# Two graph layers in one kernel: layer norms on ScalarE, their scale and shift vectors folded into weights or applied on GpSimd, and later weights loaded one by one

## The chip, the cores and the metric

The kernel runs on one core of a Trainium2 chip. The core has TensorE (PE) for matrix products, which accumulate in PSUM; VectorE (DVE), ScalarE (ACT) and GpSimd (POOL) for elementwise work; and SyncE (SP), whose ordered queue issues every DMA of this kernel. Each engine takes its instructions in program order, and engines wait for each other by semaphores. The metric is the device time in microseconds, the median of several runs.

## The reference

There are 64 independent graphs of 256 nodes with 256 features, and an integer adjacency matrix (256 x 256) for each. Two layers follow each other; all biases are zero and all scale vectors one in the data, but the kernel computes with them.

```python
# layer 0: attention with 8 heads, masked by the adjacency value r = 0..3, then a feed-forward block
q, k = src @ Wq + bq, src @ Wk + bk                    # 8 heads of 32
attn = softmax(q k^T / sqrt(32))
out  = sum over r of (attn * (adj == r)) @ (src @ Wv[r] + bv[r])
x  = ln(src + out @ Wo + bo) * g1 + beta1
x  = ln(x + gelu(x @ W1 + b1) @ W2 + b2) * g2 + beta2   # 256 -> 1024 -> 256
# layer 1: two graph-attention products (softmax over axis 1), then a feed-forward block
h  = gat(gat(x, adj, W1, a1), adj, W2, a2)             # scores leaky_relu, adj <= 0 masked
h  = ln(x + h) * g_ln1 + b_ln1
y  = ln(h + relu(h @ w_ff1 + b_ff1) @ w_ff2 + b_ff2) * g_ln2 + b_ln2
```

So a graph has four layer norms. `ln(x)` is `(x - mean) / sqrt(var + eps)` over the 256 features of a node.

## The kernel before

A graph is worked on as a whole: 256 nodes are two chunks of 128 partitions, and everything is float32 but the masks. Class `Graph` splits one graph into some 190 named steps, each a method that issues one or a few instructions. The table `PLACES` gives every step a place in time on a scale on which graphs follow each other every `PERIOD` = 60 units, and a table covers some seven such periods. At the end all steps of all 64 graphs are sorted by place and issued in that order. So the program order of every engine is written out by hand or by a planner, some seven graphs are in flight at once, and what counts in the steady state is the order of the places modulo 60. Units of the table are not microseconds.

The steps that matter here, with `m` for a half of the heads, `h` for a head, `c` for a chunk:

- Attention: `load` (features and adjacency), `cast`, `jT` (a transposing DMA), `xT` (DVE transpose), `qk`, `qkc`, `s` (PE, 32-row tiles), `max` (DVE), `exp` (ACT), `rec`, `nrm` (ACT), `eT` (DVE transpose into `sq`), `eW` and `eR` (the transposed tile through a DRAM scratch and back), `ec` (ACT copy to PSUM), `pm` (DVE product with three masks), `pl` (GpSimd product with the fourth), `v` and `vc`, `po` (PE, 32-column tiles), `oT`, `wo`, `ya`.
- Norm 1 to 4: `st` (DVE statistics), `rt` (power -1/2 on GpSimd), `ln` (DVE). Norm 1 works on tile `y`, norms 2 and 3 on `ffa_res`, norm 4 on `ffb_res`. Norm 1 is followed by the feed-forward block `a`, norm 2 by the graph attention, norm 3 by the feed-forward block `b`, norm 4 by `store`.
- Feed-forward blocks (`a` with Gelu, `b` with Relu): `aT, aW, aR` (transposed input through DRAM), `ar` (GpSimd: residual plus bias row), `au0` to `au3` (PE, products with `W1`), `ax0` to `ax3` (ACT: bias and Gelu), `ad0` to `ad7` (PE, products with `W2`), `ae` (DVE: residual); `b` likewise.
- Graph attention: `hT, hW, hR`, `ga0, ga1` with copies `gac0, gac1`, `ipA` (PE: a row spread over partitions), `zA` (ACT), `zlA, zmA, zxA` (DVE), `zeA` (ACT, Exp), `zdA` (DVE), `h10, h11` with copies `h1c0, h1c1`, the same again from `ipB` to `zdB`, then `h2` and `h2a`.

Products of PE other than `s`, `ad` and `bd` go to PSUM tiles of one tag with two buffers, taken in turn: `ps_mm` (`qk`, `v`, `po`, `wo`, `ga`, `ip`, `h1`, `h2`, `au`, `bu`). A product can start only when the one before the last has been copied out by ACT or DVE.

The norm of before is two passes over each chunk on DVE:

```python
nc.vector.scalar_tensor_tensor(yc, yc, self.mv[:, c, 0:1], self.gain, op0=ALU.subtract, op1=ALU.mult)   # L289
nc.vector.scalar_tensor_tensor(yc, yc, self.rs[:, c:c + 1], self.shift, op0=ALU.mult, op1=ALU.add)      # L293
```

The weights that are needed first (`Wq`, `Wk`, `Wv`) are loaded ahead of everything, together with the features of graphs 0 and 1. All later ones (33 DMAs: `wo`, both feed-forward blocks, the graph-attention weights, vectors) are issued in one go at the place of `jT` of graph 0. `gat_weights`, which combines the graph-attention weights on PE and DVE, has place 120.

Of the kernel before, what the change touches and what calls it, by code (L numbers as in the profile page):

```python
# [9 lines left out]
F32 = mybir.dt.float32  # L10
# [7 lines left out]
P = 128  # L18
# [6 lines left out]

PERIOD = 60.0
PLACES = {
    "load": -11.99, "cast": -4.6, "xT": -2.51, "jT": 7.74, "qk0": 12.06, "qkc0": 12.47, "mask0": 35.2,
    "qk1": 41.83, "mask4": 42.97, "qkc1": 43.93, "s0": 50.23, "max01": 52.59, "max00": 53.97,
    "exp00": 59.92, "exp01": 60.39, "rec01": 63.35, "nrm01": 68.6, "max02": 70.93, "eT01": 71.05,  # L30
    "max03": 74.95, "v00": 75.04, "mask1": 75.2, "exp02": 75.84, "rec02": 76.61, "exp03": 76.62,
    "s1": 77.63, "mask2": 78.13, "nrm02": 78.17, "vc00": 81.45, "rec00": 83.14, "rec03": 85.5,
    "eW01": 87.08, "nrm03": 87.16, "eT02": 87.32, "eR01": 90.18, "max12": 91.51, "eW02": 92.34,
    "nrm00": 93.28, "max11": 93.62, "exp12": 93.89, "eT03": 95.13, "eR02": 96.16, "rec12": 96.86,
    "eT00": 97, "exp11": 97.55, "nrm12": 97.77, "v01": 98.23, "ec01": 98.98, "max10": 100.89,
    "vc01": 101.13, "exp10": 102.04, "max13": 102.21, "y": 102.21, "rec11": 102.55, "pm01": 102.88,
    "eW03": 102.97, "mask3": 103.29, "rec10": 103.36, "nrm11": 103.84, "ec02": 104.67, "eT12": 104.67,
    "eW00": 104.68, "v10": 104.89, "eT11": 105.49, "pl01": 105.96, "eR00": 106.25, "vc10": 106.55,
    "pm02": 107.2, "exp13": 107.77, "nrm10": 110.66, "rec13": 112.27, "pl00": 112.6, "pl02": 117.17,
    "v11": 117.37, "ec00": 117.67, "eR03": 117.75, "vc11": 118.97, "pm00": 121.14, "eW11": 121.82,  # L40
    "eR11": 122.22, "eW12": 125.9, "ec03": 128.07, "pm03": 128.9, "eT10": 129.4, "pl03": 131.19,
    "nrm13": 132.88, "eR12": 133.75, "eW10": 135.15, "ec11": 135.58, "po0": 137.43, "oT0": 138.17,
    "eT13": 138.22, "pm11": 140.7, "eR10": 141.05, "ec10": 143.46, "yb": 143.7, "pl11": 144.31,
    "eW13": 144.38, "pm10": 144.52, "pl10": 145.72, "ec12": 145.91, "eR13": 149, "pl12": 149.19,
    "pm12": 150.57, "ec13": 151.58, "pm13": 153.57, "pl13": 158.31, "po1": 158.56, "oT1": 159.13,
    "wo": 166.08, "ya": 168.05, "st1": 173.82, "rt1": 178.3, "ln1": 181.37, "aT": 186.38, "aW": 188.07,
    "aR": 190.12, "ar": 199.24, "au0": 199.52, "au1": 201.67, "ax0": 202.72, "ax1": 203.71, "au2": 206.84,
    "ax2": 207.11, "ad0": 208.42, "au3": 209.92, "ad1": 210.58, "ax3": 211.3, "ad2": 212.42, "ad3": 213.46,
    "ad4": 214.51, "ad5": 214.81, "ad6": 216.46, "ad7": 216.67, "ae": 218.37, "st2": 219.27, "rt2": 220.84,
    "ln2": 221.17, "hT": 221.8, "hW": 225.17, "hR": 225.65, "ga0": 227.46, "gac0": 229.51, "ga1": 231.81,  # L50
    "gac1": 232.91, "ipA": 233.38, "zA": 233.55, "zlA": 234.68, "zmA": 236.37, "zxA": 236.64, "zeA": 238.87,
    "zdA": 239.62, "h10": 246.26, "h11": 246.44, "h1c0": 246.81, "h1c1": 247.31, "ipB": 247.55,
    "zB": 248.29, "zlB": 256.22, "zmB": 256.91, "zxB": 258.84, "zeB": 259.12, "zdB": 261.65, "h2": 265.36,
    "h2a": 266.13, "st3": 268.5, "rt3": 268.87, "ln3": 273, "bT": 277.62, "bW": 280.27, "bR": 280.43,
    "bu0": 283.46, "bx0": 284.14, "bd0": 292.07, "bu1": 295.49, "bx1": 298.81, "bu2": 302.43, "bu3": 303.37,
    "bd1": 303.83, "bx2": 304.64, "bx3": 306.29, "bd2": 306.63, "bd3": 308.89, "bd4": 312.76, "bd5": 314.98,
    "bd6": 316.39, "br": 317.09, "bd7": 320.72, "be": 323.55, "st4": 352.74, "rt4": 364.85, "ln4": 370.31,
    "store": 411.06,
}

# [11 lines left out]
def kernel(  # L72
# [52 lines left out]
    def issue_loads():  # L125
        for t, src in loads:
            nc.sync.dma_start(t, src)
        loads.clear()

    def weight(w, name, mixed=False):  # L130

        k, n = w.shape[0] // P, w.shape[1]
        t = const.tile([P, k, n], F32, name=name)
        if mixed:
            mixed_rows(t, w)
        else:
            loads.append((t, w.rearrange("(k p) n -> p k n", p=P)))
        return t

    def mixed_rows(t, w):  # L140
        for a in range(A):
            loads.append((t[a::A], w.rearrange("(k a x) n -> a x k n", a=A, x=S)[a]))

# [10 lines left out]
    def load_front(g):  # L154

        xin = fp.tile([P, KD, N // S, S], F32, tag="xin", name=f"xin{g}", bufs=1)
        xs = x[g].rearrange("(b y) (k a x) -> a y k b x", y=S, a=A, x=S)
        for a in range(A):
            nc.sync.dma_start(xin[a * S:(a + 1) * S], xs[a])
        adi = fp.tile([P, C, N], I32, tag="adi", name=f"adi{g}", bufs=1)  # L160
        nc.sync.dma_start(adi, adj[g].rearrange("(c p) d -> p c d", p=P))
        return xin, adi
# [13 lines left out]
    issue_loads()  # L176
    loaded[1] = load_front(1)
# [7 lines left out]
    w1, b1_c = weight(W1, "w1", mixed=True), colvec(b1, FF, "b1_c")  # L185
    w2, b2_r = weight(W2, "w2"), rowvec(b2, D, "b2_r")
# [12 lines left out]
    f1, bf1_c = weight(w_ff1, "f1", mixed=True), colvec(b_ff1, FF, "bf1_c")  # L199
    f2, bf2_r = weight(w_ff2, "f2"), rowvec(b_ff2, D, "bf2_r")  # L200
    gl2_r, bl2_r = rowvec(g_ln2, D, "gl2_r"), rowvec(b_ln2, D, "bl2_r")

# [61 lines left out]

    class Norm:


        def __init__(self, gain, shift, name):
            self.gain, self.shift, self.name = gain, shift, name
# [15 lines left out]

        def apply(self):
            for c in range(C):
                yc = self.y[:, c, :]
                nc.vector.scalar_tensor_tensor(yc, yc, self.mv[:, c, 0:1], self.gain,  # L289
                                               op0=ALU.subtract, op1=ALU.mult)  # L290
            for c in range(C):
                yc = self.y[:, c, :]
                nc.vector.scalar_tensor_tensor(yc, yc, self.rs[:, c:c + 1], self.shift,  # L293
                                               op0=ALU.mult, op1=ALU.add)

    class Ffn:


        def __init__(self, wa, ba, func, wb, row, name):
            self.wa, self.ba, self.func, self.wb, self.row, self.name = wa, ba, func, wb, row, name  # L300
            self.x = Transposed(f"{name}_T", bp, "sT", 3)
            self.ps = {}

        def residual(self, src):
            self.r = bp.tile([P, C, D], F32, tag="res", name=f"{self.name}_res", bufs=4)
            nc.gpsimd.tensor_tensor(self.r, src, bc(self.row, [P, C, D]), ALU.add)
# [25 lines left out]
    class Graph:  # L332
# [147 lines left out]
        def residual_bias(self):  # L480
            nc.gpsimd.tensor_tensor(self.y, self.y, bc(bo_r, [P, C, D]), ALU.add)
# [87 lines left out]
        def operations(self):  # L569
# [3 lines left out]
            self.ffa = Ffn(w1, b1_c, AF.Gelu, w2, b2_r, f"ffa{g}")  # L573
            self.ffb = Ffn(f1, bf1_c, AF.Relu, f2, bf2_r, f"ffb{g}")
# [26 lines left out]
            for n, f, src in (("a", self.ffa, lambda: self.y), ("b", self.ffb, lambda: self.ffa.r)):  # L601
                ops[f"{n}T"] = lambda f=f, src=src: f.x.squares(src())
                ops[f"{n}W"], ops[f"{n}R"] = f.x.write, f.x.read
                ops[f"{n}r"] = lambda f=f, src=src: f.residual(src())
                for i in range(KF // 2):
                    ops[f"{n}u{i}"] = lambda f=f, i=i: f.up(2 * i)
                    ops[f"{n}x{i}"] = lambda f=f, i=i: f.act(2 * i)
                for i in range(KF):
                    ops[f"{n}d{i}"] = lambda f=f, i=i: f.down(i // 4, 2 * (i % 4))
                ops[f"{n}e"] = f.end  # L610
            for n, gain, shift, src in (("1", g1_r, be1_r, lambda: self.y), ("2", g2_r, be2_r, lambda: self.ffa.r),
                                        ("3", gl1_r, bl1_r, lambda: self.ffa.r),
                                        ("4", gl2_r, bl2_r, lambda: self.ffb.r)):
                norm = Norm(gain, shift, f"x{n}_{g}")
                ops[f"st{n}"] = lambda norm=norm, src=src: norm.stats(src())
                ops[f"rt{n}"] = norm.root
                ops[f"ln{n}"] = norm.apply
# [21 lines left out]
    plan = [(PLACES["jT"], len(PLACES), issue_loads), (2 * PERIOD, len(PLACES), gat_weights)]  # L639
# [36 lines left out]
```

## Time and profile before

| | value |
|---|---|
| time, median of 3 runs | 3756.78 us (3755.02 to 3757.12) |
| span of the profiled execution | 3744.0 us |
| mean granted TensorE clock | 0.989 |
| HBM traffic | 243 MB read, 201 MB written, 119 GB/s over the span |
| first store, last store issued | 310.8 us, 3740.8 us |

The page gives the busy time of each engine as a share of the span. It says how much work an engine has, not whether somebody waits for it; for that there are the waits and the timeline. A matmul record of float32 is half a product, since each product is issued as two. A row such as `x8` in the timeline is a run of eight records, and the time between the starts of two rows is what the first one cost on PE. The costliest groups on the four engines, from the page's list:

| line | engine, tile | count | busy us | mean ns |
|---|---|---|---|---|
| L450 | DVE `pm` | 512 | 891.7 | 1742 |
| L455 | GpSimd `pl` | 512 | 597.5 | 1172 |
| L326 | PE `ffb_po` | 2048 | 513.6 | 379 |
| L428 | ACT `e` (Exp) | 1024 | 473.4 | 470 |
| L438 | ACT `e` (normalise, in place) | 1024 | 462.0 | 503 |
| L306 | GpSimd `ffb_res` (residual plus row) | 64 | 84.1 | 1313 |

### The profile page before, as it was taken

The numbers are of one execution on the slowest core, as the hardware profiler recorded it, in microseconds if no ns is written. First come the engines' busy times: TensorE is split into PE (matmuls) and PEld (weight loads), VectorE is DVE, ScalarE is ACT, GpSimd is POOL, SyncE is SP. The second block draws the span as 40 slices with busy tenths as digits, with TensorE's granted clock in tenths as the row PEclk, the third lists the DMA queues.
The fourth block names the chain that finished last, engine by engine and source line by source line (L and its number), as shares of the span: only waits on it lengthen the run. The fifth ranks groups of instructions, "written<-read, shape, count | busy, mean of one in ns | idle before, by whom it ended". The sixth has DMA issues, their size and how long they took to land.

```text
span 3744.0 us, 65142 instructions
## 1 busy us (share of the span) xinstructions
PE 3614.4 (97%) x22808; PEld 2687.0 (72%) x22808; DVE 3246.3 (87%) x5896; ACT 2217.7 (59%) x6145; POOL 1548.2 (41%) x1350
## 2 busy tenths in 40 slices
PE   5999999999999999999999999999999999999997
PEld 3677777777777777777777777777777777777775
DVE  4889888988898898898889888988988988998884
ACT  3666656655656666666656566656666665666642
POOL 3444344443443443443444444434434434444430
PEclk7999999999999999999999999999999999999998
DMA  6444344344444443443443443444444434444331
GB/s 177 125 130 125 112 130 129 114 129 121 123 123 124 127 122 123 127 124 117 128 123 113 132 127 115 130 121 123 125 123 125 124 120 127 125 123 127 118 102 34
DMA packets 808568, 457.44 MB, mean 122 GB/s; under 512 B 332976, under 2 KB 717616, under 8 KB 808240
## 3 DMA queue, kind: packets, MB, share of 16 engines
q1 hardware_dynamic: 808240, 453.27, 41.2%
q8 instruction: 181, 2.97, 0.3%
q14 instruction: 147, 1.20, 0.1%
HBM read 243.42 MB, written 201.33 MB: 119 GB/s over the span
## 4 chain that ended last, share of the span: by engine, by line
PE 52%; DVE 35%; DMA 5%; issue 5%; ACT 2%; SPq 1%; POOL 0%; DVEq 0%; POOLq 0%; ACTq 0%
PE ffb_po L326 10%; PE ffa_ps L312 7%; PE po L467 6%; DVE pm L450 6%; PE v_ps L399 6%; PE ffb_ps L312 5%; DVE nmax L420 5%; DVE ffa_res L293 4%; DVE st_x L276 4%; PE s L415 4%; DVE eT_sq L241 3%; PE h_ps L546 3%; PE h_ps L560 3%; PE qk_ps L380 3%; DMA hT<-hT_d 3%
## 5 line engine op out<-in xcount | busy, mean ns | idle before, releaser
L455 POOL TENSOR_TENSOR pl<-rell,eT 128x512 f32<-128x512 bf16 x512 | 597.5, 1172 | 969.9 <-PE po L467 517.4
L450 DVE TENSOR_TENSOR pm<-rel,pe 128x1536 f32<-128x1536 uint8 x512 | 891.7, 1742 | 100.4 <-PE po L467 83.0
L284 POOL TENSOR_TENSOR rs_x<-ve_x,nhalf 128x2 f32<-128x2 f32 x256 | 200.6, 791 | 940.4 <-DVE ve_x L280 936.1
L399 PE MATMUL v_ps<-wv,xT 128*128 128x512 f32 x1024 | 491.1, 602 | 34.7 <-DVE v L406 23.8
L326 PE MATMUL ffb_po<-f,ffb_h 128*128 128x256 f32 x2048 | 513.6, 379 | 0.6 <-ACT ffb_h L319 0.6
L312 PE MATMUL ffb_ps<-ffb_T,f 128*128 128x256 f32 x2048 | 489.5, 383 | 21.7 <-DMA ffb_T<-ffb_T_d 10.7
L428 ACT ACTIVATE e<-s,nmax 128x256 f32<-128x256 f32 x1024 | 473.4, 470 | 60.8 <-DVE nmax L420 54.3
L312 PE MATMUL ffa_ps<-ffa_T,w 128*128 128x256 f32 x2048 | 490.0, 382 | 0.7 <-DMA ffa_T<-ffa_T_d 0.7
L438 ACT ACTIVATE e<-e,rden 128x256 f32<-128x256 f32 x1024 | 462.0, 503 | 45.3 <-DVE rden L433 45.3
L312 PEld LDWEIGHTS ffb_ps<-ffb_T,f 128*128 128x128 f32 x2048 | 380.0, 190 | 119.3 <-DVE v L406 32.7
L326 PE MATMUL ffa_po<-w,ffa_h 128*128 128x256 f32 x2048 | 462.9, 379 | 0.0
L326 PEld LDWEIGHTS ffb_po<-f,ffb_h 128*128 128x128 f32 x2048 | 384.6, 190 | 76.8 <-issue 28.7
L312 PEld LDWEIGHTS ffa_ps<-ffa_T,w 128*128 128x128 f32 x2048 | 384.0, 190 | 71.6 <-issue 21.0
L326 PEld LDWEIGHTS ffa_po<-w,ffa_h 128*128 128x128 f32 x2048 | 389.3, 190 | 52.8
L420 DVE TENSOR_REDUCE nmax<-s 128x2 f32<-128x512 f32 x512 | 345.6, 676 | 80.2 <-PE s L415 80.2
L319 ACT ACTIVATE ffa_h<-ffa_ps,b_c 128x256 f32<-128x256 f32 x512 | 214.6, 470 | 283.4 <-PE ffa_ps L312 283.2
L241 DVE STREAM_TRANSPOSE eT_sq<-e 128x512 f32<-128x512 f32 x512 | 348.2, 693 | 26.3 <-DMA eT_d<-eT_sq 23.4
L467 PE MATMUL po<-pm,v 128*32 128x256 f32 x6144 | 363.9, 384 | 7.2 <-DVE pm L450 4.7
L446 ACT COPY pe<-eT 128x512 f32<-128x512 f32 x512 | 304.7, 595 | 49.6 <-DMA eT<-eT_d 29.2
L399 PEld LDWEIGHTS v_ps<-wv,xT 128*128 128x128 f32 x1024 | 190.3, 191 | 193.3 <-issue 123.6
L467 PEld LDWEIGHTS po<-pm,v 128*32 128x32 f32 x6144 | 189.4, 110 | 190.6 <-issue 57.9
L473 ACT COPY oT<-po 128x256 f32<-128x256 f32 x128 | 47.6, 372 | 447.4 <-PE po L467 447.4
(97 smaller groups left out, 5690.4 us busy)
## 6 DMA issues: line engine op xcount, KB each, us to landing
eT_d<-eT_sq SPq DMA_DIRECT2D x512, 256.0 KB, 3.3
eT<-eT_d SPq DMA_DIRECT2D x512, 256.0 KB, 2.9
xin<-in_x_dram SPq DMA_DIRECT2D x256, 64.0 KB, 3.2
adi<-in_adj_dram SPq DMA_DIRECT2D x64, 256.0 KB, 3.3
y<-in_x_dram SPq DMA_DIRECT2D x64, 256.0 KB, 3.1
ffa_T_d<-ffa_T_sq SPq DMA_DIRECT2D x64, 256.0 KB, 2.0
ffa_T<-ffa_T_d SPq DMA_DIRECT2D x64, 256.0 KB, 2.8
hT_d<-hT_sq SPq DMA_DIRECT2D x64, 256.0 KB, 2.0
```

The costliest lines, as they stand in the source:

```text
L241: nc.vector.transpose(self.sq.rearrange("p a c k y -> p (c k) a y"), src.rearrange("p c (k a x) -> p (c k) a x", k=KD, a=A))
L312: nc.tensor.matmul(p[:, f - f0, :], self.wa[:, k, f * P:(f + 1) * P], self.x.nodes(k), start=(k == 0), stop=(k == KD - 1))
L319: nc.scalar.activation(self.h[:, f, :], self.ps[f0][:, f - f0, :], self.func, bias=self.ba[:, f:f + 1])
L326: nc.tensor.matmul(self.p[:, c, :], self.h[:, f, c * P:(c + 1) * P], self.wb[:, f, :], start=(f == 0), stop=(f == KF - 1))
L399: nc.tensor.matmul(p, self.xT[:, k, jc * P:(jc + 1) * P], wv[:, k, m].rearrange("p r n -> p (r n)"), start=(k == 0), stop=(k == KD - 1))
L420: nc.vector.tensor_reduce(self.nmax[m, h], self.s4[m][h].rearrange("p (c n) -> p c n", c=C), AX.X, ALU.max, negate=True)
L428: nc.scalar.activation(e[:, ic, :], self.s4[m][h][:, ic * N:(ic + 1) * N], AF.Exp, bias=self.nmax[m, h][:, ic:ic + 1], accum_out=self.den[ ...
L438: nc.scalar.activation(e[:, ic, :], e[:, ic, :], AF.Copy, scale=self.rden[m, h][:, ic:ic + 1])
L446: nc.scalar.copy(self.pe[m, h], self.et[m, h].t.rearrange("p b c k y -> p (b c k y)"))
L450: nc.vector.tensor_tensor(self.pm[m, h], self.rel.rearrange("p r b c k y -> p r (b c k y)"), bc(self.pe[m, h], [P, R - 1, C * N]), ALU.mult)
L455: nc.gpsimd.tensor_tensor(self.pm_l[m, h], self.rel_l.rearrange("p b c k y -> p (b c k y)"), self.et[m, h].t.rearrange("p b c k y -> p (b ...
L467: nc.tensor.matmul(po[hp, :], self.v[m][:, jc, r, hp], w, start=(r == 0 and jc == 0), stop=(r == R - 1 and jc == C - 1))
```

## The change

It has four parts. First, the norm itself moves to ACT: a small DVE step `nb` computes -mean x rs, and `ln` becomes one Identity activation a chunk with `rs` as scale and `nb` as bias. Second, scale and shift: for norms 1 and 3, which feed a feed-forward block, a new function `ffn_weights` multiplies the rows of the first weight by the scale vector (ACT) once, and adds the product of shift vector and weight to the bias (PE, DVE); the residual of the block gets them in two GpSimd steps, `ag` (times scale) and `ar` (plus bias and shift row). For norms 2 and 4 two GpSimd steps follow, `lg` (times scale) and `lb` (plus shift). Third, the later loads (49 now) are issued one by one, `LOAD_STEP` = 3 places apart from the place of `jT` of graph 0, and the features of graph 1 are no longer loaded ahead. Fourth, `PLACES` is a new table, so every engine has a new order; the preparation of weights has places 195 (`a`), 200 (graph attention) and 255 (`b`).

It is meant to take work off DVE, the engine with the most work after PE, and to keep the burst of loads out of the way of the first graph's transfers.

```diff
-        for t, src in loads:
-            nc.sync.dma_start(t, src)
-        loads.clear()
+    def issue_load():
+        t, src = loads.pop(0)
+        nc.sync.dma_start(t, src)
...
-    issue_loads()
-    loaded[1] = load_front(1)
+    while loads:
+        issue_load()
...
+    def ffn_weights(w, b, gain, shift, row, shift_row, name):
+        p = mm_tile([P, KF], f"{name}_b_ps")
+        for f in range(KF):
+            for k in range(KD):
+                nc.tensor.matmul(p[:, f:f + 1], w[:, k, f * P:(f + 1) * P], shift[:, k],
+                                 start=(k == 0), stop=(k == KD - 1))
+        nc.vector.tensor_tensor(b, p, b, ALU.add)
+        for k in range(KD):
+            nc.scalar.activation(w[:, k], w[:, k], AF.Copy, scale=gain[:, k])
+        nc.vector.tensor_tensor(row, row, shift_row, ALU.add)
...
+    def times(out, t, row):
+        nc.gpsimd.tensor_tensor(out, t, bc(row, [P, C, D]), ALU.mult)
+    def plus(t, row):
+        nc.gpsimd.tensor_tensor(t, t, bc(row, [P, C, D]), ALU.add)
...
+        def offset(self):
+            self.nb = small.tile([P, C], F32, tag="nb", name=f"nb_{self.name}")
+            nc.vector.scalar_tensor_tensor(self.nb, self.mv[:, :, 0], -1.0, self.rs, op0=ALU.mult, op1=ALU.mult)
         def apply(self):
             for c in range(C):
                 yc = self.y[:, c, :]
-                nc.vector.scalar_tensor_tensor(yc, yc, self.mv[:, c, 0:1], self.gain,
-                                               op0=ALU.subtract, op1=ALU.mult)
-            for c in range(C):
-                yc = self.y[:, c, :]
-                nc.vector.scalar_tensor_tensor(yc, yc, self.rs[:, c:c + 1], self.shift,
-                                               op0=ALU.mult, op1=ALU.add)
+                nc.scalar.activation(yc, yc, AF.Identity, bias=self.nb[:, c:c + 1], scale=self.rs[:, c:c + 1])
...
         def residual(self, src):
             self.r = bp.tile([P, C, D], F32, tag="res", name=f"{self.name}_res", bufs=4)
-            nc.gpsimd.tensor_tensor(self.r, src, bc(self.row, [P, C, D]), ALU.add)
+            times(self.r, src, self.gain)
+        def residual_row(self):
+            plus(self.r, self.row)
...
+LOAD_STEP = 3.0
+FFA_PLACE, GAT_PLACE, FFB_PLACE = 195.0, 200.0, 255.0
...
-    plan = [(PLACES["jT"], len(PLACES), issue_loads), (2 * PERIOD, len(PLACES), gat_weights)]
+    plan = [(PLACES["jT"] + i * LOAD_STEP, len(PLACES), issue_load) for i in range(len(loads))]
```

Of the table, the steps around the graph attention of one graph and the feed-forward block `a` of the next, as places modulo 60, in order (other steps between them are left out). Before:

```text
PE   h10 6.3, h11 6.4, ipB 7.6, qk0 12.1, v00 15.0, po0 17.4, s1 17.6, au0 19.5, bd7 20.7, au1 21.7, h2 25.4, au2 26.8, au3 29.9
ACT  zB 8.3, qkc0 12.5, exp02 15.8, exp03 16.6, oT0 18.2, zeB 19.1, ax0 22.7, ax1 23.7, ax2 27.1, ax3 31.3, exp12 33.9
```

After:

```text
PE   po0 35.6, s1 35.9, h10 38.1, h11 39.5, au0 39.7, ipB 40.3, bd6 40.9, bd7 42.5, au1 46.0, v01 46.5, au2 49.8, ad0 50.1, au3 53.1, h2 53.2
ACT  h1c0 39.4, h1c1 39.9, zB 41.1, ax0 45.4, ec10 46.0, ax1 47.1, zeB 50.2, ax2 51.8, ec12 52.4, nrm00 55.8, ax3 56.4, exp12 57.6
```

## The prediction

> **What bounds the kernel now.** I read the page's busy shares and chain first, then TensorE's waits, then the busy time by stretches, and last the timelines of TensorE (PE) and ScalarE (ACT) over one round of the steady state.
>
> ```profile
> PE 3614.4 (97%) x22808; PEld 2687.0 (72%) x22808; DVE 3246.3 (87%) x5896; ACT 2217.7 (59%) x6145; POOL 1548.2 (41%) x1350
> ...
> PE 52%; DVE 35%; DMA 5%; issue 5%; ACT 2%; SPq 1%; POOL 0%; DVEq 0%; POOLq 0%; ACTq 0%
> ```
>
> PE is busy 97% of the span. DVE's 35% of the chain tempts one to believe that relieving DVE pays, so the next question is how long PE waits for anybody (waits of PE, whole span):
>
> ```profile
> PE ga_wps L497 <- DMA hT<-hT_d: 28.1, 25, 8.6
> PE v_ps L399 <- DVE v L406: 23.8, 1, 23.8
> PE v_ps L399 <- ACT kT L391: 10.9, 55, 0.4
> PE ffb_ps L312 <- DMA ffb_T<-ffb_T_d: 10.7, 4, 9.7
> PE ffb_ps L312 <- DVE v L406: 9.6, 33, 0.5
> ```
>
> Only the repeated waits (25, 55, 33 times) belong to the steady state, and they are short; the single 23.8 us belongs to the start. The stretches say when PE idles (columns: length, PE, PEld, DVE, ACT, POOL busy, PE clock, DMA share, GB/s):
>
> ```profile
> 20.00:40.00 20.00, 6.98 (x32) 3.69 (x30) 4.65 (x11) 7.36 (x26) 4.73 (x4) 0.76 0.93 207
> 40.00:60.00 20.00, 7.17 (x22) 3.10 (x23) 7.97 (x13) 5.39 (x16) 5.56 (x4) 0.59 0.72 209
> ...
> 1000.00:1500.00 500.00, 493.26 (x3148) 367.32 (x3148) 446.77 (x809) 306.54 (x852) 210.94 (x183) 1.00 0.41 122
> ```
>
> In the steady state PE idles 6.7 us of 500. The output product `wo` of one graph starts at 250.88 us and that of the graph 57 later at 3485.45: a round takes 56.75 us, and 64 rounds are 3632 of the 3744 us. But "busy" hides small waits, so I took a round apart in PE's timeline:
>
> ```profile
> 1502.70 1.15 PE L415 MATMUL s<-kT,qT 32*128 32x256 f32 x16
> 1503.78 1.14 PE L497 MATMUL ga_wps<-gext,hT 128*128 128x260 f32 x4
> ...
> 1509.29 1.89 PE L312 MATMUL ffb_ps<-ffb_T,f 128*128 128x256 f32 x8
> 1511.48 1.99 PE L312 MATMUL ffb_ps<-ffb_T,f 128*128 128x256 f32 x8 [0.31 <-DVE v L406]
> 1513.32 1.03 PE L326 MATMUL ffb_po<-f,ffb_h 128*128 128x256 f32 x4
> ```
>
> Undisturbed, 8 matmul records of 256 columns take 1.73 us from start to start (4 take 0.865, `v` 1.72, `po` 3.46, `s` 0.865). A whole round at that pace sums to 53.97 us. The rest, 2.78 us, has two parts. Where PE changes to the 32-wide tiles of `s` and `po` and back, rows run late by 0.1 to 0.2 us: 0.48 for an `s` alone, 0.35 for a `po` alone, 0.55 for a `po` with `s` right behind; before has one of each, 1.38 us. The other 1.40 us is waiting: `ffb_ps` above for DVE to empty a buffer, `v_ps` for ACT, `ga_wps` for a transfer. So all that a relieved DVE can give is about 1.4 us a round, 90 us in all.
>
> **What the Trainium skill says.** "ScalarE: Activation LUTs", section "Table sets: the hidden batching unit": functions come in sets, a change of set is a load, and cheap ones (copy, identity) are in every set. The trace agrees: Identity and Copy stand among the Exp with no load, and loads occur only between Exp and Gelu. Its section "What ACT_TABLE_LOAD costs" gives 1283 ns and a drain of 1380 ns after it. The load has 1283 ns here too, but ACT goes on at once, so I take 1.28 us and no drain:
>
> ```profile
> 1528.97 0.19 ACT L532 ACTIVATION_READ_ACCUMULATOR gb_z<-gb_z,gb_max 128x1 f32 x1
> 1529.18 1.28 ACT L319 ACT_TABLE_LOAD   x1
> 1530.69 0.84 ACT L319 ACTIVATE ffa_h<-ffa_ps,b_c 128x256 f32<-128x256 f32 x2 [0.23 <-PE ffa_ps L312]
> ```
>
> The load starts when the instruction ahead has ended; it does not wait for PE. "GPSIMD Engine Reference", section "Specifications": GpSimd's SBUF interface is shared with VectorE operations that read two SBUF inputs. The trace agrees: the pair at L293 takes 0.87 us alone and 1.78 us beside a GpSimd product. "TensorE: Matmul & The Clock Gate", section "What's actually happening": an idle PE falls to half its clock. The trace agrees: after the 23.8 us wait `v_ps` takes 3.53 us instead of 1.88.
>
> **The change part by part.**
>
> *Engine load.* DVE loses the two passes of the norms: at L293 110.3+77.2+57.0+55.6 = 300 us, at L289 65.7+60.8+57.2+54.4 = 238. It gains 256 small `nb` at 0.17 us (the `ve` row where undisturbed), 44. Net -494 us, to about 74%. ACT gains 512 Identity at 0.45 us (L438, in place, same shape): 230 us. GpSimd gains six 128x512 products or sums a graph at 1.28 (L306): 492 us, to 55%. None of the three becomes the bound.
>
> *Table loads.* The new order puts `zeB` (Exp) between `ax1` and `ax2` (Gelu). The built program has 255 loads in place of 129: 126 x 1.28 = 162 us more of ACT, to some 70%. What counts is the place. In before the load to Gelu runs while PE computes `au0`. In after, ACT's order is `h1c1, zB, load, ax0`, and PE's is `au0, ipB, bd6, bd7, au1`. PE's products share two PSUM buffers in turn, so `au1` must wait until `ax0` has emptied that of `au0`. With `ipB` starting at 0: `zB` starts at 0.42 (as after `ips` at 1505.62 and 1516.78), ends at 1.26; load to 2.55; `ax0` to 3.41; `au1` at 3.46. PE has finished `ipB, bd6, bd7` at 0.22+0.865+0.865 = 1.95. A new wait of 1.51 us, with 0.1 for the restart 1.61 us a round. Queued behind `au1` on PE are `v01`, `au2` and all else.
>
> *The rest of the round.* I walked PE's order through with these durations, and ACT's, DVE's and GpSimd's queues beside it. `po1, s0` and `po0, s1` now stand together: 2 x 0.55 = 1.10 us. Everything else arrives in time: `v` buffers are emptied at once because DVE has gaps, and `hT`, behind the two new GpSimd passes `lg2, lb2`, is in place about 1.1 us ahead of `ga0` if it takes the 6.1 us that before shows from transpose to product. The least slack is 0.25 to 0.3 us (`bu1` behind `ya`, `ipA` behind `gac1`, `au0` behind `h1c0`). Sum: 53.97 + 1.10 + 1.61 = 56.68; the walk with its roundings gives 56.77. That is the round of before. The old waits are gone, a new one takes their place.
>
> *Start.* Before sends its 33 later loads in one burst from 17.0 to 43.5 us, ahead of the first attention transfers; `po` of graph 0 starts at 77.8. Spread out, one every few transfers, the first attention transfer goes at about 25 us. With 3 us per landing and the weights between, the fourth of the first half lands near 50: `po` near 54, and `wo` of graph 0 at about 79 in place of 100.2. Then the graph-attention weights (8 us, they used to fill a gap), 32 one-column matmuls with their waits (4 us twice) eat into it, while fewer idle gaps give some back: I carry 14 us of the 21 to the steady state. The scaling of `w1` and `f1` on ACT, about 1 us a piece, lies ahead of need.
>
> *End.* `lg2, lb2` and `lg4, lb4` put 2 x 1.28 us on the last graph's chain, and `nb` plus two Identity (1.0) replace four passes (1.75): about +2.6 for each of two norms; an earlier `au0` behind `wo` returns some 3. Net +2.
>
> Sum: 3756.8 + 64 x 0.02 - 14 + 2 = 3746 us.
>
> **The rivals.** *More waits (slower).* The slacks of 0.3 us are eaten by GpSimd and DVE slowing each other down, or by SP's ordered queue. Before had 1.4 us of such waits; 0.45 us in after give 57.2: 3756.8 + 64 x 0.45 - 14 + 2 = 3774 us. For it: the doubled L293 row, GpSimd at 55%. Against it: the operation most hit is the one removed. *The relief pays in full (much faster).* If the wait at `au1` does not arise and DVE's slack removes the old ones, a round is 53.97 + 1.10 + 0.1: 55.2, 3756.8 - 64 x 1.55 - 12 = 3646 us. For it: the 35% of DVE in the chain. Against it: the 1.28 us load, which nothing visible can hide. *No gain at the start (same).* The loads still queue ahead of the attention transfers on SP, or later preparation eats all: 3746 + 14 = 3760 us.
>
> **How the numbers follow.** Forecast 0.45, more waits 0.27, full relief 0.13, no gain at the start 0.15. The forecast's middle lies 11 us below before; with its spread of about 10 us a third of it falls within 0.2% (7.5 us). Faster: 0.30 + 0.13 = 0.43. Same: 0.13 + 0.12 = 0.25. Slower: 0.32. The range runs from 3690, between the full relief and the forecast, to 3790, where waits of 0.7 us a round would end; a tenth is left out on each side.
>
> **What would show it.** Right: in the steady state PE waits once a round, about 1.5 us, at `ffa_ps` for ACT `ffa_h`; waits of PE for `v` on DVE are gone; 255 table loads; a round of 56.6 to 56.9; `po` of graph 0 near 54. Wrong: a round below 56 (the wait is hidden), or above 57 with waits at `ga_wps` for `hT` or at `h_ps` for DVE; or a first `po` still behind 70.

## The result and the profile after

The kernel after takes 3654.78 us (median of 4 runs, 3653.86 to 3659.45), the kernel before on the same chip 3755.9 us: a ratio of 0.9736, 95% interval 0.9719 to 0.9752. The forecast was 3746 us with a range from 3690 us, so the change gained 101 us where I expected 11. The profiled spans are 3744.0 and 3652.1 us, with a clock of 0.989 in both. The profiled execution of before took 3745.8 us, 10 us less than the median, so the profiles below account for 92 us of the gain.

The busy shares and the chain of the kernel after, from its page:

```profile
PE 3567.7 (98%) x22872; PEld 2712.3 (74%) x22872; DVE 2703.1 (74%) x5132; ACT 2630.4 (72%) x6787; POOL 2012.5 (55%) x1734
...
PE 94%; DMA 3%; DVE 1%; ACT 1%; SPq 1%; issue 0%; POOL 0%; POOLq 0%; ACTq 0%; DVEq 0%
```

The shares of DVE, ACT and POOL came out within 3 points of what was worked out, and the chain is now almost PE alone. The busy time in stretches of the kernel after (columns as before: length, PE, PEld, DVE, ACT, POOL, PE clock, DMA share, GB/s), and all that PE waits for between 1000 and 2000 us:

```profile
20.00:40.00 20.00, 15.57 (x60) 8.02 (x56) 7.93 (x17) 10.40 (x32) 9.07 (x7) 0.75 0.79 198
40.00:60.00 20.00, 9.09 (x70) 3.36 (x70) 13.05 (x19) 7.77 (x25) 7.83 (x7) 0.66 0.63 172
...
1500.00:2000.00 500.00, 500.00 (x3225) 381.97 (x3224) 382.90 (x729) 373.23 (x964) 284.51 (x246) 1.00 0.43 126
```

```profile
PE ga_wps L534 <- DMA hT<-hT_d: 0.7, 1, 0.7
```

PE is busy for 500.00 of 500 us, and waits once in 18 rounds. A round, from one `wo` to the next, takes 55.06 us (the median; a few rounds have a short wait, so the 58 rounds in the table below average 55.12). That is 53.97 + 1.10, the undisturbed products and the changes of tile width that the prediction summed, with nothing added. What is missing is the new wait at `au1`, 1.61 us with its restart. PE's timeline of the kernel after shows the place, and ACT's timeline the load:

```profile
1541.98 1.89 PE L349 MATMUL ffa_ps<-ffa_T,w 128*128 128x256 f32 x8
1543.71 0.38 PE L546 MATMUL gb_ips<-ident,gb_wh 128*128 128x128 f32 x2
1543.92 1.89 PE L363 MATMUL ffb_po<-f,ffb_h 128*128 128x256 f32 x8
1545.65 1.89 PE L349 MATMUL ffa_ps<-ffa_T,w 128*128 128x256 f32 x8
1547.38 1.88 PE L436 MATMUL v_ps<-wv,xT 128*128 128x512 f32 x4
```

```profile
1544.19 0.84 ACT L553 ACTIVATE gb_z<-gb_ips,gb_wh 128x256 f32<-128x256 f32 x2 [1.63 <-PE gb_ips L546]
1545.04 1.28 ACT L356 ACT_TABLE_LOAD   x1
1546.34 0.84 ACT L356 ACTIVATE ffa_h<-ffa_ps,b_c 128x256 f32<-128x256 f32 x2
```

The rows on PE are `au0`, `ipB`, `bd6` with `bd7`, `au1`, `v01`. `au1` starts at 1545.65, without a wait, while ACT is still loading its table and before `ax0` begins (1546.34). So `au1` does not write to the buffer of `au0`. There are only two, so it has the buffer of `ipB`, which `zB` emptied by 1545.03. `v01` then gets `au0`'s buffer.

Where the 91.9 us between the two spans are, by the starts of `wo` (first, fourth, 62nd and last graph):

| stretch | before | after | difference |
|---|---|---|---|
| start to `wo` of graph 0 | 100.16 | 81.71 | -18.4 |
| to graph 3 | 150.72 | 165.54 | +14.8 |
| 58 rounds, to graph 61 | 3291.09 | 3196.87 | -94.2 |
| to graph 63 | 99.25 | 95.49 | -3.8 |
| from there to the end | 102.78 | 112.49 | +9.7 |

The rounds carry the whole gain. The earlier start is more than given back in the next three rounds and at the end.

### The profile page after: what moved, and what is told of

The parts are those of the page before. It is cut to its first block, busy times and chain, and to the rows that moved or that the text cites. A ratio compares the mean times of both kernels' runs of the same rounds, so it can differ in the third digit from the quotient of the medians.

```text
span 3652.1 us, 65487 instructions
## 1 busy us (share of the span) xinstructions
PE 3567.7 (98%) x22872; PEld 2712.3 (74%) x22872; DVE 2703.1 (74%) x5132; ACT 2630.4 (72%) x6787; POOL 2012.5 (55%) x1734
## 4 chain that ended last, share of the span: by engine, by line
PE 94%; DMA 3%; DVE 1%; ACT 1%; SPq 1%; issue 0%; POOL 0%; POOLq 0%; ACTq 0%; DVEq 0%
PE po L504 12%; PE ffb_ps L349 12%; PE ffb_po L363 12%; PE ffa_ps L349 12%; PE v_ps L436 12%; PE ffa_po L363 12%; PE qk_ps L417 6%; PE s L452 4%; PE h_ps L583 3%; PE ga_wps L534 3%; PE h_ps L597 3%; PE wo_ps L524 3%; DMA eT_d<-eT_sq 1%; DMA hT<-hT_d 0%; PE gb_ips L546 0%
## 5 line engine op out<-in xcount | busy, mean ns | idle before, releaser
L318 POOL TENSOR_TENSOR rs_x<-ve_x,nhalf 128x2 f32<-128x2 f32 x256 | 180.2, 704 | 976.0 <-DVE ve_x L314 686.2
L363 PE MATMUL ffb_po<-f,ffb_h 128*128 128x256 f32 x2048 | 493.5, 379 | 0.0
L349 PE MATMUL ffb_ps<-ffb_T,f 128*128 128x256 f32 x2048 | 458.0, 382 | 16.0 <-DMA ffb_T<-ffb_T_d 16.0
L349 PEld LDWEIGHTS ffb_ps<-ffb_T,f 128*128 128x128 f32 x2048 | 393.0, 192 | 71.4 <-issue 12.4
L443 DVE TENSOR_TENSOR v<-v_ps,bv_r 128x512 f32<-128x512 f32 x256 | 174.3, 681 | 349.0 <-PE v_ps L436 218.4
L269 DVE STREAM_TRANSPOSE eT_sq<-e 128x512 f32<-128x512 f32 x512 | 357.5, 698 | 19.4 <-DMA eT_d<-eT_sq 10.8
L356 ACT ACTIVATE ffb_h<-ffb_ps,bf_c 128x256 f32<-128x256 f32 x512 | 215.0, 473 | 109.4 <-PE ffb_ps L349 109.3
```

The costliest lines, as they stand in the source:

```text
L269: nc.vector.transpose(self.sq.rearrange("p a c k y -> p (c k) a y"), src.rearrange("p c (k a x) -> p (c k) a x", k=KD, a=A))
L349: nc.tensor.matmul(p[:, f - f0, :], self.wa[:, k, f * P:(f + 1) * P], self.x.nodes(k), start=(k == 0), stop=(k == KD - 1))
L363: nc.tensor.matmul(self.p[:, c, :], self.h[:, f, c * P:(c + 1) * P], self.wb[:, f, :], start=(f == 0), stop=(f == KF - 1))
```

## The experiments

Theory: the steady state is fast because `au1` takes the buffer that `zB` frees. The main rivals were that the forecast's walk was wrong in another place, and that either the new order or the relief of VectorE is enough by itself. Ratios are to the kernel before on the same chip.

**1. The buffers strictly in turn** (`in_turn`). Two tags with one buffer each replace one tag with two:

```diff
-    ps_mm = ctx.enter_context(tc.tile_pool(name="ps_mm", bufs=2, space=bass.MemoryType.PSUM))
+    ps_mm = ctx.enter_context(tc.tile_pool(name="ps_mm", bufs=1, space=bass.MemoryType.PSUM))
...
+    turn = [0]
     def mm_tile(shape, name, dt=F32):
-        return ps_mm.tile(shape, dt, tag="mm", name=name)
+        turn[0] ^= 1
+        return ps_mm.tile(shape, dt, tag=f"mm{turn[0]}", name=name)
```

> The kernel after, with TensorE's product buffers handed out strictly in turn; in every round this swaps the buffers of h1 (two), au1 and v01 and of no other product. Theory 'free buffer' (after is fast because au1 takes the buffer that zB frees and so need not wait for ax0 behind the table load): the wait that the prediction assumed comes back, some 1.5 us once a round at ffa_ps for ffa_h, a round of about 56.6 us, in all 3745 to 3760 us. Rival 'slack elsewhere' (the walk was wrong in some other place, and the buffer does not matter): no new wait, a round of 55.1 us, 3655 us.

Measured: 3763.25 us, ratio 1.0043 (1.0026 to 1.006). The waits of PE over the whole span, and one round of its timeline:

```profile
PE ffa_ps L352 <- ACT ffa_h L359: 92.6, 64, 3.1
```

```profile
1587.24 0.38 PE L549 MATMUL gb_ips<-ident,gb_wh 128*128 128x128 f32 x2
1587.46 1.89 PE L366 MATMUL ffb_po<-f,ffb_h 128*128 128x256 f32 x8
1590.76 1.99 PE L352 MATMUL ffa_ps<-ffa_T,w 128*128 128x256 f32 x8 [1.41 <-ACT ffa_h L359]
```

The wait is there once for each graph. In the steady state PE is idle for 1.41 us by the trace; by the starts of the rows, the measure in which 1.51 was predicted, it is 1.57 (3.30 from `bd6` to `au1`, less 1.73). The round is 56.745 us (four rounds from 1502.94 to 1729.92), where the prediction had 56.68 by the sum and 56.77 by the walk. The edit changes the buffers of `h1` and `v01` too, but between 1000 and 2000 us PE waits at `au1` alone (18 times, 25.4 us). So the prediction's arithmetic was right for a kernel that takes its buffers in turn. This edit to allocation alone gives back the entire gain of the change.

**2. The order without the norms** (`order_only`). `PLACES` and the spread loads of after; in the norm the two VectorE passes of before, and no folded weights.

```diff
-                nc.scalar.activation(yc, yc, AF.Identity, bias=self.nb[:, c:c + 1], scale=self.rs[:, c:c + 1])
+                nc.vector.scalar_tensor_tensor(yc, yc, self.mv[:, c, 0:1], self.gain,
+                                               op0=ALU.subtract, op1=ALU.mult)
+            for c in range(C):
+                yc = self.y[:, c, :]
+                nc.vector.scalar_tensor_tensor(yc, yc, self.rs[:, c:c + 1], self.shift,
+                                               op0=ALU.mult, op1=ALU.add)
...
-                ops[f"lg{n}"] = lambda f=f, gain=gain: times(f.r, f.r, gain)
-                ops[f"lb{n}"] = lambda f=f, shift=shift: plus(f.r, shift)
+                ops[f"lg{n}"] = ops[f"lb{n}"] = lambda: None
```

> The order of work and the spread loads of the kernel after, but the norms as before on VectorE with gain and shift (no nb, no lg, lb, no folded weights, one residual sum). Theory 'order' (the new places removed the waits, the moved norms do nothing for the round): VectorE back at 87 to 89%, a round of 55.1 to 55.4 us, 3640 to 3670 us. Rival 'relief' (without the relief of VectorE the new order has the waits of before or more): a round of 56 to 57.5 us, 3710 to 3810 us.

Measured: 3742.38 us, ratio 0.9988 (0.998 to 0.9996); a round is 56.53 us (four rounds from 1492 us). The waits of PE over the span, then VectorE's timeline at the place:

```profile
PE ffb_ps L354 <- DVE y L533: 73.7, 61, 3.2
```

```profile
1549.71 0.87 DVE L327 SCALAR_TENSOR_TENSOR ffa_res<-ffa_res,mv_x,g_r 128x256 f32<-128x256 f32 x2
1550.50 0.87 DVE L331 SCALAR_TENSOR_TENSOR ffa_res<-ffa_res,rs_x,be_r 128x256 f32<-128x256 f32 x2
1551.30 1.74 DVE L492 TENSOR_TENSOR pm<-rel,pe 128x1536 f32<-128x1536 uint8 x1
1552.96 0.68 DVE L533 TENSOR_TENSOR y<-wo_ps,y 128x512 f32<-128x512 f32 x1
```

`ya` must empty the buffer of `wo` before `bu1` can start. The 1.6 us of norm passes ahead of it in the queue are what the change moves away; with them `bu1` waits 1.18 us a round. The order alone therefore gains almost nothing: in it the relief is worth 56.53 - 55.06 = 1.47 us a round.

**3. One place mended** (`order_ya`). As `order_only`, with `ya` ahead of `pm01` in VectorE's queue.

```diff
-    "wo": 192.72, "ya": 194.55, "st1": 197.35,
+    "wo": 192.72, "ya": 193.85, "st1": 197.35,
```

> The kernel order_only (norms on VectorE as before) with one place changed: ya, VectorE's sum that empties the buffer of wo, goes ahead of the masked product pm01 instead of behind it. Theory 'one queue place' (order_only lost its 1.47 us a round only because ya stood behind 4.4 us of VectorE's work): a round of 55.06 to 55.3 us although VectorE is still at 86%, in all 3640 to 3665 us. Rival 'VectorE is too full' (the next slack runs out at once): a round of 56 us or more, 3705 us or more.

Measured: 3725.88 us, ratio 0.9914 (0.9899 to 0.9928), a round of 56.165 us (four rounds from 1490 us). The old wait is gone, and the next one is there. The waits of PE over the span, and ACT's timeline:

```profile
PE ffb_ps L354 <- ACT ffb_h L361: 51.2, 61, 1.1
```

```profile
1550.63 0.59 ACT L488 COPY pe<-eT 128x512 f32<-128x512 f32 x1 [5.16 <-DVE pm L492]
1551.16 1.56 ACT L361 ACTIVATE ffb_h<-ffb_ps,bf_c 128x256 f32<-128x256 f32 x4
```

With `pm01` later, the ACT copy for the next head waits longer for its PSUM buffer (5.16 us, 4.55 in `order_only`), and `bx0` stands behind that copy. Of 1.47 us a round 0.37 came back in these rounds; over the 58 rounds of the table above it is less, 0.27 (56.60 to 56.33). VectorE, busy for 440 us of 500 here, has too little slack for this order; the rival holds.

**4. The norms in the old order** (`norms_only`, `norms_13`). `PLACES` and the burst of loads of before. In the first all four norms are as after, with `nb` right behind `rt` and `lg`, `lb` right behind `ln`:

```diff
+    "rt2": 220.84, "nb2": 220.84, "ln2": 221.17, "lg2": 221.17, "lb2": 221.17, "hT": 221.8,
```

> The order of work and the burst of loads of the kernel before, with the norms on ScalarE and GpSimd and the folded weights as after. Theory 'relief' (VectorE's slack removes the waits): a round of 53.97 + 1.38 + about 0.2 = 55.5 us, 3670 to 3690 us. Rival 'order' (VectorE's load was not what TensorE waited for): a round of 56.5 us or more, 3740 us or more; with the two GpSimd passes ahead of hT a longer wait at ga_wps, up to 3830 us.

In the second only norms 1 and 3 are as after, with `nb` right ahead of `ln`:

```diff
+                if n in "24":
+                    ops[f"nb{n}"] = ops[f"lg{n}"] = ops[f"lb{n}"] = lambda: None
+                    ops[f"ln{n}"] = lambda norm=norm, gain=gain, shift=shift: norm.apply_whole(gain, shift)
```

> The order of work and the burst of loads of before; only the first and the third norm on ScalarE with their gain and shift folded, the second and the fourth on VectorE as before, so that no GpSimd pass stands ahead of hT (in norms_only VectorE stopped 3.8 us a round there); nb stands directly ahead of its norm. Theory 'the relief pays also in the old order, norms_only only failed at hT': a round of 55.4 to 56.2 us, 3680 to 3735 us. Rival 'the relief pays only in an order written for it': a round of 56.6 us or more, 3755 us or more.

Measured: 4098.89 us, ratio 1.0934 (1.0918 to 1.0951), and 4024.03 us, ratio 1.0718 (1.07 to 1.0736). My upper end for the first was 3830 us, and its wait was expected at `ga_wps`: both were wrong. In `norms_only` VectorE itself stops at `hT` for the GpSimd passes, with everything behind it in its queue, as its timeline shows:

```profile
1573.39 0.71 DVE L268 STREAM_TRANSPOSE hT_sq<-ffa_res 128x512 f32<-128x512 f32 x1 [3.76 <-POOL ffa_res L296]
```

From there it goes by way of `rec`, `nrm` and the copy of `kT` on ACT to a wait of 3.12 us at `v_ps`. In `norms_13` there is no such pass, and ACT stops instead, since the Identity of norm 1 stands in ACT's queue ahead of the Relu `bx2`. ACT's timeline, then PE's:

```profile
1507.34 1.09 ACT L326 ACTIVATE y<-y,nb_x,rs_x 128x256 f32<-128x256 f32 x2 [1.89 <-DVE nb_x L321]
1508.34 1.54 ACT L363 ACTIVATE ffb_h<-ffb_ps,bf_c 128x256 f32<-128x256 f32 x4
```

```profile
1509.21 3.17 PE L590 MATMUL h_ps<-ga_wh,ga_z 128*128 128x258 f32 x8 [2.65 <-ACT ffb_h L363]
1512.17 1.59 PE L370 MATMUL ffb_po<-f,ffb_h 128*128 128x256 f32 x4
```

So a norm on ACT is a hand-over DVE, GpSimd, DVE, ACT, and in an in-order queue it holds up whatever follows if it is issued too early. I tried only these two ways of placing it; with other places the old order might take the norms better, and that was not tried.

**5. The loads in a burst** (`burst`). The kernel after with all later loads at the place of `jT`, and graph 1's inputs ahead of them.

```diff
-    plan = [(PLACES["jT"] + i * LOAD_STEP, len(PLACES), issue_load) for i in range(len(loads))]
+    plan = [(PLACES["jT"], len(PLACES), burst)]
...
+    loaded[1] = load_front(1)
```

> The kernel after with the later weights in one burst behind the first transposes of the adjacency, and graph 1's inputs ahead of them, as before. The round stays at 55.06 us. Theory 'the lead of the start is lost in the first rounds' (18.5 us of lead at the first output product, 3.6 us at the fourth): 3655 to 3665 us. Rival 'the spread loads are worth what the first output product shows': 3670 to 3676 us.

Measured: 3673.37 us, ratio 0.9801 (0.9786 to 0.9816), span 3671.7 us. The round stays at 55.06 us, `wo` of graph 0 starts at 102.16 us and that of graph 3 at 266.79 us, each some 20 us later than in after. My theory fell: the lead that the spread loads win is kept. What the kernel after gives back between graphs 0 and 3 has another cause, and `burst` pays it too.

**6. The preparation of weights moved** (`gat_early`, `gat_121`, `early_prep`, `order_ya_gat`). In after PE works 3.5 us for `ffa_b_ps`, 10.3 us for the graph-attention weights and 3.5 us for `ffb_b_ps`, all behind the first `wo`. In these kernels the nine loads of the graph-attention weights go first, and the preparation goes to other places: `GAT_PLACE` is 150 in `gat_early` and `order_ya_gat` (which is `order_ya` besides) and 121 in `gat_121`. `early_prep` moves all three:

```diff
-FFA_PLACE, GAT_PLACE, FFB_PLACE = 195.0, 200.0, 255.0
+FFA_PLACE, GAT_PLACE, FFB_PLACE = 187.0, 121.0, 264.9
```

> The kernel after with the preparation of the graph-attention weights (10.3 us on TensorE behind the first output product) moved ahead of the first head product, where TensorE waits 7.6 us for masks, and the nine loads it needs moved to the front of the later loads. Theory 'the preparation cost the start its lead': 6 to 10 us less than after, 3645 to 3650 us. Rival 'the first rounds are held by something else': as after, 3655 us, or more, where VectorE's copies for the preparation delay the masks.

> As gat_early, but the preparation of the graph-attention weights stands at place 121, ahead of the transpose eT00 on which VectorE stops 9.4 us for a transfer (in gat_early TensorE waited 14.0 us for the copy of gw2T behind that stop). Theory 'it was only the place': the first output product at 84 us as in after and the fourth some 8 to 10 us earlier than after's 249.5, in all 3646 to 3651 us. Rival 'the first rounds are held by something else' (a lead won early is lost again): 3655 to 3660 us.

> As gat_121, and the two folds of the norms' scale and shift into the weights moved to where TensorE waits in after: the first to place 187 (before the second half of qk of graph 2, 5.1 us), the second to place 264.9 (before the graph-attention product of graph 0, 4.5 us). If the preparation is what the start pays: 5 to 7 us less than gat_121, 3640 to 3645 us. Rival: the weights land too late for it, or the lead is lost again: as gat_121 or more.

> Both edits together: norms on VectorE in the order of after, ya ahead of pm01, the graph-attention weights prepared early. If both theories hold: round 55.06 to 55.3 us, no folding of weights, a shorter drain by 2 to 3 us, in all 3630 to 3655 us, the fastest of all. If VectorE is too full: 3700 us or more.

> The kernel after on the same chip, for the comparison: 3655 us, within 0.3%.

Measured, with the starts of `wo` in the profile:

| kernel | us | ratio (95%) | graph 0 | graph 3 |
|---|---|---|---|---|
| `after_again` | 3658.69 | 0.9737 (0.9722 to 0.9751) | 84.13 | 249.51 |
| `gat_early` | 3658.43 | 0.9739 (0.9724 to 0.9753) | 89.96 | 251.69 |
| `gat_121` | 3654.70 | 0.9749 (0.9733 to 0.9765) | 86.38 | 247.33 |
| `early_prep` | 3649.31 | 0.9735 (0.972 to 0.9749) | 88.90 | 242.94 |
| `order_ya_gat` | 3731.22 | 0.9925 (0.9908 to 0.9941) | 89.80 | 252.28 |

In `gat_early` PE stood 14.0 us at `gu_ps`, since VectorE's copy of `gw2T` stood behind other work in its queue, a stop of 4.4 us for an ACT copy among it. In `gat_121` that is gone, and still at most some 2 us of the 10.3 arrive at graph 3, no more than two profiles of after differ there (247.25 and 249.51). In `early_prep` the matmuls of `ffa_b_ps` fill a wait, but run there at half pace (PE's timeline):

```profile
72.03 6.68 PE L224 MATMUL ffa_b_ps<-be_c,w 128*128 128x1 f32 x32 [3.67 <-DVE v L443]
78.57 2.05 PE L417 MATMUL qk_ps<-xT,wq 128*128 128x256 f32 x4
```

With all three moves graph 3 comes 4.3 to 6.6 us earlier than in the two profiles of after, out of 17.3 us of work. `early_prep` is 5.4 us faster than `gat_121` on the same chip, and all of its runs lie below those of `gat_121`, as its expectation had it. But the ratios do not tell it from after, so no version here is known to beat that. `order_ya_gat` fares as `order_ya` does: its round is VectorE's. What is left of PE's waits in the first 260 us of `early_prep`, besides 8.1 us for the first weights, is at most a few us each, at `s`, `po`, `v`, `ffa` and `ga_wps`; which of them bounds the first rounds stays open.

## Why the prediction was wrong, and where it was right

- **The step that failed** is "PE's products share two PSUM buffers in turn, so `au1` must wait until `ax0` has emptied that of `au0`". With a tag of two buffers the pool gave `au1` the one that was released first in program order: `zB` (place 41.1 in the round) stands ahead of `ax0` (45.4). The timeline of after shows `au1` at work before `ax0` starts, and `in_turn` puts the wait and the whole 107 us of span back (3652.1 to 3759.3). That the rule is "released first" I infer from this place and from `h1`, whose buffers also change in `in_turn`; that `au1` does not take `au0`'s buffer is shown. The description of the kernel before ("two buffers, taken in turn") has the same error.
- **"The 1.28 us load, which nothing visible can hide"** was the same error once more. `ipB`, `bd6` with `bd7`, and `au1` (0.22 + 1.73 + 1.73 us) stand on PE between `au0` and `v01`, the first that needs `au0`'s buffer. They cover the load: `ax0` ends at 1547.18, `v01` starts at 1547.38. The 126 more loads cost ACT the 162 us that were worked out, and PE nothing.
- **The round otherwise was right.** 53.97 + 1.10 = 55.07 against 55.06 measured. "All that a relieved DVE can give is about 1.4 us a round" was right in size: 1.47 in experiment 2. What was not seen is that the order had been written for the relieved VectorE, so neither part gains alone: the order 0.1%, the relief a loss of 7 to 9% in the two forms tried.
- **"The least slack is 0.25 to 0.3 us (`bu1` behind `ya`)"** named the place that breaks when VectorE is loaded again (experiment 2).
- **Engine load** was right: VectorE lost 543 us (494 predicted), GpSimd gained 464 (492), ACT 413 (392). Two terms were too small: an Identity with two pointer operands takes 0.549 us (281.1 us over 512), not 0.45, and `nb` 0.26 us (66.8 over 256), not 0.17. VectorE's other work got some 72 us shorter, which the prediction did not have; why stays open.
- **Start**: `wo` of graph 0 at 81.71 us, predicted 79; spreading the loads alone is worth some 20 us (experiment 5). "14 us of the 21 to the steady state" was wrong: 3.6 us are left at graph 3. The preparation on PE, 17.3 us here and 16 in the prediction, was to cost 7 net, since fewer idle gaps were thought to give the rest back; they did not. Experiment 6 shows that a quarter to a third of it is had when it is moved into waits.
- **End**: predicted +2 us, measured +9.7. `order_only`, without the moved norms, needs 109.6 us from the last `wo` to the end, so +6.8 belong to the order and +2.9 to the norms. The 2.9 are norm 4 alone: from the last product to the end it is 10.1 us in after, 7.1 in before and 7.2 in `order_only`. That is close to "about +2.6 for each", although the terms given for it (2.56 + 1.0 - 1.75) make only 1.8; a cost of norm 2 does not show. "An earlier `au0` behind `wo` returns some 3" does not show: with the order PE works longer there, 76.5 us in after and 79.3 in `order_only` against 71.6, at a granted clock of 0.86 in place of 0.90, and waits about as long (25.9 and 23.1 us against 24.1). One such place is the block of `bu0` to `bu3` behind a transfer, 9.93 us to the next row where 6.92 would be the pace. Before stops for the same transfer, and its next row of eight records then lasts 3.38 us instead of 1.89, so this place explains only a part. PE's timeline of after:

```profile
3624.97 10.10 PE L349 MATMUL ffb_ps<-ffb_T,f 128*128 128x256 f32 x32 [9.86 <-DMA ffb_T<-ffb_T_d]
3634.90 7.07 PE L363 MATMUL ffb_po<-f,ffb_h 128*128 128x256 f32 x32
```

- **The rivals**: "the relief pays in full", at 0.13, was the case, with 3646 us and a round of 55.2. It was held small on the strength of the failed step alone. Its -12 us for start and end were not had (-3.6 at graph 3, +9.7 at the end), more than the 9 us by which after stays above its 3646. Of the third rival, "later preparation eats all" came close to being so: 3.6 of the 21 us are left. Of the signs named beforehand, "a round below 56 (the wait is hidden)" was the one that appeared.

## What to carry to other kernels

Before a wait for a buffer is priced, look up which buffer the allocator hands out, not which one turn and turn about would give: the built program's waits name the instruction that frees it, and the wait predicted here (1.68 us a round with its restart, 107 us in all) exists or not by that alone. Where an edit and a new order come together, price them together: a relieved engine gives time only in an order that issues the moved work late enough for its inputs, and an order written for the relieved engine breaks at its smallest slack without it. An earlier first result is not an earlier end: follow it to the third or fourth round before it is counted.

## What the runs showed of the hardware

A wait of PE of 1.41 us (`in_turn`) or 1.18 us (`order_only`) leaves the next product at its pace: 1.83 us from start to start, with 1.73 undisturbed. The waits in experiment 4 are longer, and most of them cost more than their length, since the clock granted to PE falls to half. Not all do. The wait of `norms_13` at 1509.21, shown above, has a twin of the same length in another round; below it are PE's stretches behind both (columns as before, PE clock third from the end):

```profile
1084.03 2.01 PE L590 MATMUL h_ps<-ga_wh,ga_z 128*128 128x258 f32 x8 [2.63 <-ACT ffb_h L363]
```

```profile
1084.03:1088.00 3.97, 3.97 (x19) 3.49 (x20) 1.03 (x1) 2.76 (x8) 3.08 (x3) 1.00 0.30 104
1509.89:1513.30 3.41, 3.41 (x10) 2.68 (x9) 0.00 (x0) 1.24 (x3) 2.46 (x2) 0.50 0.41 134
```

At 1084.03 the eight records keep their pace (1.85 us to the next row); at 1509.21 they take 2.96 us. Between 250 and 3700 us of `norms_13` and `norms_only` the clock records of the traces change only on a fixed grid of 3.41 us, and a fall lasts one or two steps of it. In this time the two kernels have 110 waits of 2.2 to 3.4 us at these places (`h_ps` in the first, `v_ps` in the second). Where at most 1.94 us of the wait lay within one step of the grid (16 waits), the clock did not fall; where 1.99 us or more did (94 waits), it was at half in the next step, without exception. So it is the place of the wait on the grid that decides, and a single wait of up to 1.9 us was safe here. The price of a fall is seen in the 24 records behind a wait in `norms_13`: 6.5 to 6.8 us with it, 5.09 without. The granted clocks over the span are 0.968 and 0.963.

The Trainium skill, "TensorE: Matmul & The Clock Gate", section "What's actually happening", puts the fall to half clock after at least one idle window of about 3.4 us. The length of the step agrees, 3.41 us; but a step with some 2.0 us of idle time was enough here, so for that the measurement decides.
